# Two attention layers and two routed feed-forward layers on one core: deviation rows by half batch, weight places taken one by one, statistics made ahead by unit

## The chip, the cores and the metric

The kernel runs on one core of a Trainium2 chip. A core has five engines that each work through their own list of instructions in order: TensorE (PE, matrix products and transposes; its weight loads are listed apart as PEld), VectorE (DVE), ScalarE (ACT), GpSimd (POOL) and SyncE (SP), which here issues nearly all DMA transfers. [...]The metric is the time of one execution in microseconds (us) on the device. The kernel before took 4159.81 us (median of 3 runs, 4158.99 to 4161.47).

## The reference, cut to what matters

Four layers work on 4 batches of 4096 tokens with 128 channels. The first two (a state-space scan and a hypergraph layer) are not touched by the change. The other two each consist of an attention and a feed-forward part, both of which read the tokens normalised over their channels:

```python
t = t + _L2_attn_ref(_ln_t(t), L2_attn_W, L2_attn_b)              # causal linear attention
t = t + _L2_ffn_ref(_ln_t(t), gate_w, gate_b, weight1, weight2)
t = t + _L3_attn_ref(_ln_t(t), Wq, bq, Wk, bk, Wv, bv)            # windowed, without softmax
t = t + _L3_ffn_ref(_ln_t(t), gate_w, gate_b, weight1, weight2)

def _ln_t(v, eps=1e-5):
    m = mean(v, axis=-1); s = var(v, axis=-1)
    return (v - m) / sqrt(s + eps)

def ffn(x):                       # 64 experts, 8 tokens each per batch
    probs = softmax(x @ gate_w.T + gate_b, axis=tokens)
    topv, topi = top_k(probs per expert, 8)
    pooled = sum over k of x[topi] * topv                     # (batch, expert, channel)
    h = gelu(pooled @ weight1[expert] + bias)                 # 128 -> 512
    out = h @ weight2[expert] + bias                          # 512 -> 128
    scatter-add out * topv back to the chosen tokens
```

The weights of one feed-forward part are 64 experts times (128 x 512 + 512 x 128) numbers of 4 bytes, 32 MB.

## The kernel before, in words

The tokens of all batches lie in one on-chip tensor `X` (128 tokens by 4 x 32 blocks by 128 channels) from the end of layer 1 on. The order of the work on each engine is that of a list written out by a scheduling layer: it starts from the program's order, but moves an instruction forward into a gap when its inputs and its place are free. So what the source says of an order holds only in part; small VectorE instructions in particular are pulled far ahead.

**attn2** (layer 2, 32 units `u` of one batch and four blocks; `project(u)`, `score(u - 1)`, `attend(u - 2)`). Each unit needs the mean and the deviation of its tokens. `ln_stats` (L733) makes them for 16 blocks, four units, at a time: 16 `bn_stats` on VectorE (L737), some small operations, one Sqrt on ScalarE (L729), a reciprocal. Exp, which every unit needs (L882), and Sqrt lie in different function tables of ScalarE, so each such Sqrt among the units brings two table loads.

**attn3** (layer 3, 32 chunks `s` of one batch and four blocks; `turned(s)`, `gram(s)`, `values(s - 2)`, `mixed(s - 2)`, `put(s - 3)`). Statistics again 16 blocks at a time. Of the four normalised blocks `z` of a chunk ScalarE makes three (L1035) and VectorE one (L1037).

**tokens_done and spread.** As soon as a chunk of tokens has its final value, its `bn_stats` for the feed-forward part are made (L783); 16 blocks are a half batch. `spread` turns a finished half into deviations. Only when all four halves of a pair of batches `p` are there are they transposed, written to a scratch in HBM (L800), and read back as a row that is repeated over 64 experts for each of the two batches (L803, two reads of 1 MB): `rsb[p]`, 128 x 4096.

**ffn.** `logits(p)` works out the gate's logits of a pair in eight chunks and multiplies each by its part of `rsb[p]` (L1198). `choose(p)` marks the eight best tokens (L1215 over all 4096 tokens) and makes the weights by Exp and a product (L1222, L1223). `gather(p)` pools the tokens (L1246, L1253). The order is: `logits(0)`; the last `spread`; `logits(1)` beside `choose(0)`; `choose(1)` beside `gather(0)`; `gather(1)`. Then come 16 groups `g` of four experts: `hidden(g)` with `w1` (L1317), `turn(g - 1)`, `outputs(g - 2)` with `w2` (L1339). `w1` and `w2` of a group are 1 MB each. Five groups have a place on the chip: the first has its own (loaded during the attention), two take the place of the rows `rsb` and two that of `ch` and `ex`, the buffers of `choose`. Each of these two regions is closed as a whole before a load into it is asked for, and group `g + 5` is loaded, `w1` then `w2`, after `outputs(g)`. In layer 3 the steps also transpose `X` back (`channels`, L1360). At last the outputs are scattered into `X` (L1395, L1400; L1405, L1407) and, in layer 3, written out.

Of the kernel before, what the change touches and what calls it, by code (L numbers as in the profile page):

```python
# [41 lines left out]
class Net:  # L42
# [3 lines left out]
    def setup(self, ctx):  # L46
# [22 lines left out]
        self.scratch = [dram.tile([2 * NB, P], F32, tag=f"rs_{i}", name=f"rs_{i}") for i in range(B)]  # L69
# [662 lines left out]
    def ln_stats(self, sp, b, j0, n):  # L732

        nc, X = self.nc, self.X
        st = sp.tile([P, n, 6], F32, tag="lnst", name="lnst")
        for j in range(n):
            nc.vector.bn_stats(st[:, j, :], X[:, b, j0 + j, :])  # L737
        nm = sp.tile([P, n], F32, tag="lnnm", name="lnnm")
        nc.vector.tensor_tensor(nm, st[:, :, 1], st[:, :, 4], ALU.add)
        nc.vector.tensor_scalar(nm, nm, -0.5, None, ALU.mult)  # L740
        rs = sp.tile([P, n], F32, tag="lnrs", name="lnrs")
        self.deviations(sp, st, rs)
        return nm, rs


    def ffn_open(self, name):
# [4 lines left out]
        self.rbp = tc.tile_pool(name="frb", bufs=1, reuse_waits="tile")  # L751
        rbp = self.rbp.__enter__()
# [10 lines left out]
        self.rsb = [rbp.tile([P, N], F32, tag=f"rb{p}", name="rsb") for p in range(B // 2)]  # L763
        self.half, self.halves, self.known = {}, [], [0] * (B // 2)
# [12 lines left out]
    def tokens_done(self, b, c):  # L777
# [4 lines left out]
        for i in range(4):  # L782
            self.nc.vector.bn_stats(self.half[b][:, 4 * k + i, :], self.X[:, b, 4 * c + i, :])  # L783
# [3 lines left out]
    def spread(self, new):  # L787

        nc = self.nc
        for b, h, st in self.halves:  # L790
            p, r = divmod(b, 2)
            self.deviations(self.fsp, st, self.rsk[p][:, r, 16 * h : 16 * (h + 1)])
            self.known[p] += 1
            if self.known[p] == 4:
                pt = new()
                nc.tensor.transpose(pt[: 2 * NB, 0, :], self.rsk[p].rearrange("p r j -> p (r j)"), self.ident)
                rT = self.fsp.tile([2 * NB, P], F32, tag="rT", name="rT", bufs=2)
                nc.vector.tensor_copy(rT, pt[: 2 * NB, 0, :])
                d = self.scratch.pop()
                nc.sync.dma_start(d, rT)  # L800
                for r in range(2):
                    src = bass.AP(tensor=d.tensor, offset=d[r * NB : (r + 1) * NB, :].offset, ap=[[0, E], [1, N]])
                    nc.sync.dma_start(self.rsb[p][r * E : (r + 1) * E, :], src)  # L803
        self.halves = []

    def attn2(self):
# [8 lines left out]
        with ExitStack() as ctx:  # L815
# [28 lines left out]
            state, stats = {}, {}  # L844

            def norms(b, g):
                nm, rs = self.ln_stats(sp, b, G * g, 16)
                nb = sp.tile([P, 16], F32, tag="lnnb", name="lnnb")
                nc.vector.tensor_tensor(nb, nm, rs, ALU.mult)
                nc.vector.tensor_scalar(nb, nb, 1.0, None, ALU.add)  # L850
                stats[b] = rs, nb
                self.spread(new)

            def project(u):

                b, g = units[u]
                if g % 4 == 0:
                    norms(b, g)
                rs, nb = stats[b]
# [3 lines left out]
                for i in range(G):  # L863
                    k = G * (g % 4) + i
                    x, r, m = X[:, b, G * g + i, :], rs[:, k : k + 1], nb[:, k : k + 1]
# [67 lines left out]
            units = [(2 * p + r, g) for p in range(B // 2) for g in range(NB // G) for r in range(2)]  # L933
            S = {}
            for u in range(len(units) + 3):
# [4 lines left out]
                if u < len(units):  # L940
                    project(u)
                if 0 <= u - 1 < len(units):
                    score(u - 1)
# [8 lines left out]
    def attn3(self):  # L952
# [11 lines left out]
        with ExitStack() as ctx:  # L964
# [46 lines left out]
            stats, zts, sums, maps = {}, {}, {}, {}  # L1011

            def norms(s):

# [461 lines left out]
```

## Time and profile before

| | us |
|---|---|
| median of 3 runs | 4159.81 |
| the profiled execution | 4161.4 |
| its span (first to last instruction) | 4159.6 |
| layers 0 and 1, to the start of attn2 | 0 to 3377 |
| attn2 | 3377 to 3644 |
| ffn of layer 2: first transposes of `logits(0)` | 3642.4 |
| its first `hidden` | 3723.8 |
| its first scatter product (L1395) | 3796.4 |
| attn3, first product of a chunk | 3830 |
| ffn of layer 3: first transposes of `logits(0)` | 3970.2 |
| its first `hidden` | 4048.0 |
| its first scatter product (L1405) | 4123.5 |

Busy shares of the whole span: PE 84%, DVE 72%, POOL 59%, ACT 50%. They are an average over very different stages and say little of the last 783 us, which are all that the change touches. How to read the views: the table of stretches gives, for each stretch of time, the busy microseconds and (in brackets) the number of instructions of PE, PEld, DVE, ACT and POOL, then the clock that was granted to PE, the share of the 16 DMA engines' time that was in use and the GB/s they moved. The chain of waits is followed backward from the last instruction: a start, a duration, and what the end was waiting for in that time. A timeline line gives start, duration, engine, source line, operation and operands; in square brackets stands how long the engine had idled before it and for whom. "issue" is time for which the profile shows no cause.

### The profile page before, as it was taken

To read this page: it belongs to the slowest core of one execution; us is meant where nothing else is said; L and a number is where in the kernel's file an instruction comes from. 1 tells how busy PE (TensorE), PEld (TensorE's weight loads), DVE (VectorE), ACT (ScalarE), POOL (GpSimd) and SP (SyncE) were. 2 spreads that over 40 slices of the span, in tenths; PEclk is the share of its full clock that TensorE was granted. 3 is DMA by queue.
4 is the path that set the end of the run, shared out by engine and by line. 5 is a ranking of instruction groups with operands and counts; after the bars stand their busy time and mean duration, and the time that the engine had idled before them with its cause. 6 is when DMAs were issued, how large, how long until landed. Compare 5 with 4: busy or idle time off the path is not lost. (4 is left out here: it accounts for less than half of the span.)

```text
span 4159.6 us, 48628 instructions
## 1 busy us (share of the span) xinstructions
PE 3481.7 (84%) x17232; PEld 1949.8 (47%) x17243; DVE 2985.6 (72%) x4632; ACT 2078.7 (50%) x3519; POOL 2460.1 (59%) x1242
## 2 busy tenths in 40 slices
PE   6878857888888788888967888887998969988988
PEld 2323323444543434445333344543566457855854
DVE  5888889988766899976679988764641077655764
ACT  4556554455644545555444455642124078742941
POOL 5999879888778788877869888773000020001300
PEclk8988978899999889999987999998999989998999
DMA  3445544455446444543644545356111420055037
GB/s 101 149 146 153 157 112 128 132 143 147 115 144 185 111 128 129 153 129 99 218 115 123 137 138 145 114 162 209 59 71 44 139 85 1 22 168 185 22 119 287
DMA packets 263014, 532.71 MB, mean 128 GB/s; under 512 B 22474, under 2 KB 24946, under 8 KB 262258
## 3 DMA queue, kind: packets, MB, share of 16 engines
q1 hardware_dynamic: 254834, 519.08, 42.5%
q10 hardware_dynamic: 7936, 10.52, 0.7%
q8 instruction: 136, 2.23, 0.2%
q14 instruction: 108, 0.88, 0.1%
HBM read 451.80 MB, written 77.73 MB: 127 GB/s over the span
## 5 line engine op out<-in xcount | busy, mean ns | idle before, releaser
L291 POOL TENSOR_TENSOR db<-dx,bt 128x1024 f32<-128x1024 f32 x512 | 1203.2, 2353 | 331.7 <-DVE hs L309 216.0
L309 DVE TENSOR_TENSOR_SCAN hs<-hs,carry,db 128x512 f32<-128x512 f32 x812 | 1037.1, 1285 | 176.9 <-ACT hs L303 94.8
L303 ACT ACTIVATE hs<-dl,A 128x512 f32<-128x512 f32 x1024 | 706.5, 692 | 740.1 <-DVE ho L319 684.9
L326 POOL TENSOR_TENSOR ho_s<-ho_s,ho 128x1024 f32<-128x1024 f32 x288 | 677.9, 2354 | 13.6 <-DVE ho L319 13.0
L504 PE MATMUL ps_g<-xn 128*128 128x512 f32 x1152 | 603.7, 655 | 96.9 <-DVE inc L507 73.3
L319 DVE TENSOR_TENSOR ho<-hs,bt 128x1024 f32<-128x1024 f32 x464 | 564.5, 1217 | 1.6
L527 PE MATMUL ps_ed<-xs,inc 128*128 128x258 f16 x4096 | 516.4, 287 | 18.4 <-ACT inc L520 8.6
L527 PEld LDWEIGHTS <-inc 128*128 128x128 fp8e4 x4096 | 419.0, 103 | 136.3 <-issue 61.1
L507 DVE SCALAR_TENSOR_TENSOR inc<-ps_g,hcl,hb 128x512 fp8e4<-128x512 f32 x576 | 421.8, 739 | 36.9 <-PE ps_g L504 21.5
L504 PEld LDWEIGHTS ps_g<-xn 128*128 128x128 f32 x1152 | 216.1, 204 | 414.5 <-DVE inc L507 180.6
L347 PE MATMUL ps_y<-ho,cst 128*128 128x512 f32 x512 | 274.1, 679 | 108.0 <-POOL ho L315 90.7
L627 PE MATMUL ps_v<-inc_v,es 128*128 128x512 fp8e4 x1536 | 343.3, 383 | 19.3 <-DMA bt<-bcd 17.3
L627 PEld LDWEIGHTS <-es 128*128 128x128 f16 x2048 | 202.7, 99 | 289.7 <-issue 65.1
L520 ACT CAST inc<-ps_t 128x512 fp8e4<-128x512 f32 x448 | 232.2, 599 | 93.7 <-PE ps_t L516 93.5
L229 PE MATMUL ps_c<-xt,wc 128*128 128x512 f32 x512 | 235.4, 614 | 13.0 <-DVE inc L507 6.8
L347 PEld LDWEIGHTS ps_y<-ho,cst 128*128 128x128 f32 x512 | 105.1, 215 | 268.5 <-POOL ho L315 121.6
L533 ACT COPY ed<-ps_ed 128x129 f32<-128x129 f32 x128 | 34.1, 266 | 383.5 <-PE ps_ed L527 383.5
L534 DVE TENSOR_TENSOR ed<-ps_ed,ed 128x129 f32<-128x129 f32 x128 | 36.8, 288 | 212.7 <-ACT ed L533 209.7
L543 POOL TENSOR_TENSOR ed<-ed,rdeg 128x512 f32<-128x512 f32 x32 | 33.3, 1040 | 250.0 <-DVE rdeg L539 250.0
L309 DVE TENSOR_TENSOR_SCAN hs<-hs,db 128x512 f32<-128x512 f32 x116 | 141.4, 1225 | 53.5 <-POOL db L291 42.5
L229 PEld LDWEIGHTS ps_c<-xt,wc 128*128 128x128 f32 x512 | 100.0, 198 | 140.6 <-issue 119.7
L1161 POOL CAST b1h<-b 128x512 bf16<-128x512 f32 x2 | 1.2, 614 | 270.2 <-DMA b<-in_L_ffn_weight 270.2
(321 smaller groups left out, 5493.9 us busy)
## 6 DMA issues: line engine op xcount, KB each, us to landing
bt<-bcd SPq DMA_DIRECT2D x512, 512.0 KB, 5.1
inc<-inc SPq DMA_DIRECT2D x192, 256.0 KB, 2.8
inc_v<-inc SPq DMA_DIRECT2D x96, 512.0 KB, 6.4
w<-in_L_ffn_weight SPq DMA_DIRECT2D x32, 1024.0 KB, 11.5
w2f<-in_L_ffn_weight SPq DMA_DIRECT2D x32, 1024.0 KB, 11.5
strip<-inc SPq DMA_DIRECT2D x84, 256.0 KB, 4.6
x<-x ACTq DMA_DIRECT2D x32, 256.0 KB, 5.5
xn<-x SPq DMA_DIRECT2D x32, 256.0 KB, 5.6
```

What stands on the lines that cost most here:

```text
L229: nc.tensor.matmul(s["ps"][h], wc[:, h, j, :], xt[:, j : j + T], start=j == 0, stop=j == 3)
L291: nc.gpsimd.tensor_tensor(db, s["dx"], bc(s["bt", n][:, 0, :], 2), ALU.mult)
L303: act(nc.scalar.activation(hs[:, k, :], s["dl"][:, k, :], AF.Exp, scale=A[:, k, n : n + 1]))
L309: nc.vector.tensor_tensor_scan(to[:, h, :], hs[:, h, :], db[:, h, :], init, ALU.mult, ALU.add)
L319: nc.vector.tensor_tensor(ho, hs, ct, ALU.mult)
L326: nc.gpsimd.tensor_tensor(s["sum", n // G], s["sum", n // G], ho, ALU.add)
L347: nc.tensor.matmul(s["y"][h], self.ident, t[:, h, :], start=False, stop=n == DS - 1 and k == len(terms) - 1,)
L504: nc.tensor.matmul(pq, xn[v // 4][:, v % 4 * P : (v % 4 + 1) * P], xn[c], start=True, stop=True)
L507: nc.vector.scalar_tensor_tensor(inc[:, v, :], pq, hc[:, v : v + 1], hb, ALU.subtract, ALU.is_gt, saturate=False)
L520: later(1, lambda: act(nc.scalar.copy(inc[:, v, :], pt, saturate=False)))
L527: nc.tensor.matmul(pe[:, : 2 * P + 2], inc[:, v, i * P : (i + 1) * P], xs[:, v, :], start=v == 0, stop=v == NB - 1,)
L627: nc.tensor.matmul(pv, es[:, e, k, :], inc[:, e, :], start=e == 0 and k == 0, stop=e == NB - 1 and k == 1,)
```

## The change

Three things change.

1. A finished half batch becomes its own row at once. `spread` transposes 16 columns instead of 64, writes 16 x 128 numbers and reads them back once, repeated over 64 experts (512 KB). There are four row buffers `rsb[2p + h]` of 128 x 2048, one for each half of each pair, instead of two of 128 x 4096. `logits` takes the half that its chunk lies in.
2. A load of weights takes one place when the last user of that place has ended, not when a region is closed. `w1` and `w2` are loaded by calls of their own. Groups 1 and 2 (modulo 5) take the four row buffers, group 3 takes `ch`, group 4 takes the two `ex` buffers (now two of 128 x 2048 instead of three of 128 x 1024). Group 1 is asked for after `logits(0)` and group 2 after `logits(1)` beside `choose(0)`; `w1` of group `g + 5` is asked for after `hidden(g)`, its `w2` after `outputs(g)`.
3. The attentions' statistics are asked for unit by unit. `measure(n)` makes the `bn_stats` up to unit `n`, `finish(f)` the deviations of a set of units; the sets begin at units 0, 2, 8, 16, 24 in attn2 and at 0, 1, 4, 8, ... in attn3. In attn3 VectorE makes two of the four `z` in even chunks and one in odd ones.

The compiled lists of instructions for layers 0 and 1 are the same in both kernels. In attn2 the list of ScalarE has 13 Sqrt table loads before and 10 after. In both feed-forward parts the list of SP has the two loads of group 1 ahead of the last rows' write and read.

```diff
-    def ln_stats(self, sp, b, j0, n):
-        st = sp.tile([P, n, 6], F32, tag="lnst", name="lnst")
-        for j in range(n):
-            nc.vector.bn_stats(st[:, j, :], X[:, b, j0 + j, :])
...
+    def ahead_of(self, sp, units, firsts):
+        ends = dict(zip(firsts, [*firsts[1:], len(units)]))
+        most = max(e - f for f, e in ends.items())
+        sets, ready, n = {}, {}, 0
+        def measure(upto):
+            nonlocal n
+            while n < min(upto, len(units)):
+                f = max(f for f in firsts if f <= n)
+                if f == n:
+                    st = sp.tile([P, most, 4, 6], F32, tag="lnst", name="lnst", bufs=2)
+                    sets[f] = st[:, : ends[f] - f, :, :]
+                self.block_stats(sets[f][:, n - f, :, :], *units[n])
+                n += 1
+        def finish(f):
+            if f in sets:
+                rs, nb = self.norms(sp, sets.pop(f).rearrange("p u i s -> p (u i) s"))
+                for u in range(f, ends[f]):
+                    i = 4 * (u - f)
+                    ready[u] = rs[:, i : i + 4], nb[:, i : i + 4]
...
-            self.known[p] += 1
-            if self.known[p] == 4:
-                pt = new()
-                nc.tensor.transpose(pt[: 2 * NB, 0, :], self.rsk[p].rearrange("p r j -> p (r j)"), self.ident)
-                rT = self.fsp.tile([2 * NB, P], F32, tag="rT", name="rT", bufs=2)
...
-                nc.sync.dma_start(d, rT)
-                for r in range(2):
-                    nc.sync.dma_start(self.rsb[p][r * E : (r + 1) * E, :], src)
+            pt = new()
+            nc.tensor.transpose(pt[:16, 0, :], self.rsk[p][:, r, 16 * h : 16 * (h + 1)], self.ident)
+            rT = self.fsp.tile([16, P], F32, tag="rT", name="rT", bufs=2)
+            nc.vector.tensor_copy(rT, pt[:16, 0, :])
+            d = self.scratch.pop()
+            nc.sync.dma_start(d, rT)
+            src = bass.AP(tensor=d.tensor, offset=d[0:1, :].offset, ap=[[0, E], [1, N // 2]])
+            nc.sync.dma_start(self.rsb[2 * p + h][r * E : (r + 1) * E, :], src)
...
+            measure(2)
+            finish(0)
             for u in range(len(units) + 3):
...
                     project(u)
+                    measure((5, 8, 10, 11, 12, 14, 15)[u] if u < 7 else u + 9)
+                    finish(u + 1)
+                    if u % 8 == 7:
+                        self.spread(new)
...
-                    if i:
+                    if i % 2 or (i and s % 2):
                         nc.scalar.activation(z[:, i, :], x, AF.Identity, scale=r, bias=m)
                     else:
                         nc.vector.tensor_scalar(z[:, i, :], x, r, m, ALU.mult, ALU.add)
...
+                measure((4, 6, 8)[s] if s < 3 else s + 6)
+                finish(s + 2 if s else 1)
...
-                    nc.vector.tensor_tensor(lg[:, sl], pl, rsb[p][:, sl], ALU.mult)
+                    rb = rsb[2 * p + c // 4][:, c % 4 * CH : (c % 4 + 1) * CH]
+                    nc.vector.tensor_tensor(lg[:, sl], pl, rb, ALU.mult)
...
             run(logits(0))
             self.spread(turned)
+            load(1, 0)
+            load(1, 1)
             second = logits(1)
             next(second)
             run(second, choose(0))
-            self.rbp.__exit__(None, None, None)
-            with_a = ctx.enter_context(tc.tile_pool(name="fe2", bufs=2, reuse_waits="tile"))
-            load(1)
-            load(2)
+            load(2, 0)
+            load(2, 1)
             first = gather(0)
             next(first)
             run(choose(1), first)
-            fctx.close()
-            with_b = ctx.enter_context(tc.tile_pool(name="fe3", bufs=2, side="right", reuse_waits="tile"))
-            load(3)
-            load(4)
+            for g in (3, 4):
+                load(g, 0)
+                load(g, 1)
             run(gather(1))
...
                 if g > 1:
                     outputs(g - 2)
-                    load(g + 3)
+                    if (g - 2) % 5 == 3:
+                        load(g + 3, 0)
+                    load(g + 3, 1)
                 if 0 < g <= NG:
                     turn(g - 1)
                 if g < NG:
                     hidden(g)
+                    if g % 5 != 3:
+                        load(g + 5, 0)
```

## The prediction

> **What bounds the kernel now.** The lists of layers 0 and 1 don't change, so I start with the table of stretches, cut at the stages of the last 783 us.
>
> ```profile
> 3377.00:3640.00 263.00, 241.49 (x1637) 197.79 (x1638) 194.89 (x761) 212.20 (x450) 0.00 (x0) 0.97 0.04 9
> 3662.00:3679.00 17.00, 7.17 (x50) 4.44 (x50) 11.89 (x15) 10.22 (x19) 0.00 (x0) 0.83 0.73 166
> 3679.00:3693.00 14.00, 14.00 (x75) 6.71 (x75) 11.24 (x19) 9.43 (x16) 0.00 (x0) 0.84 0.19 54
> 3724.00:3796.00 72.00, 58.77 (x750) 29.65 (x742) 13.12 (x25) 13.18 (x21) 5.19 (x16) 0.91 0.96 345
> 3830.00:3971.00 141.00, 130.00 (x969) 118.30 (x968) 101.04 (x417) 124.67 (x357) 50.12 (x70) 0.98 0.08 18
> 4048.00:4122.00 74.00, 67.14 (x863) 39.99 (x873) 23.22 (x36) 21.80 (x37) 0.63 (x2) 1.00 0.86 313
> ```
>
> Attn2 (first line) is PE's, with ScalarE behind it. In layer 2's expert groups (fourth line) the DMA share is 0.96: they run at the pace of the weights. In layer 3's (last line) PE comes first and DMA second. Attn3 (fifth line) keeps PE and ScalarE busy together. In the second line PE works 7 of 17 us and the DMA engines are busy: the rows. The chain of waits names these:
>
> ```profile
> 3662.77 2.94 DMA rs<-rT
> 3666.23 11.83 DMA rsb<-rs
> ...
> 3771.38 12.36 DMA w<-in_L_ffn_weight
> ...
> 3790.30 1.98 PE ps_eo L1339 x32
> ...
> 3990.41 11.42 DMA rsb<-rs
> ```
>
> In both feed-forward parts `logits(1)` waits for a write and a read of its rows, and the end of layer 2's groups follows the landing of the last `w1`. VectorE's timeline tells what was really lost to the rows:
>
> ```profile
> 3664.48 4.41 DVE L1215 MATCH_REPLACE8 ch<-m,lg 128x4096 f32<-128x4096 f32 x1
> ...
> 3678.18 1.29 DVE L1198 TENSOR_TENSOR lg<-ps_l,rsb 128x512 f32<-128x512 f32 x2 [4.29 <-DMA rsb<-rs]
> ...
> 3693.30 4.41 DVE L1215 MATCH_REPLACE8 ch<-m,lg 128x4096 f32<-128x4096 f32 x1
> ```
>
> It did `choose(0)` during the wait and idled 4.29 us. From one `MATCH_REPLACE8` to the next are 28.8 us; that stretch is what the rows can shorten. SP's timeline gives the weights' pace:
>
> ```profile
> 3724.95 1.23 SPq L1122 DMA_DIRECT2D w<-in_L_ffn_weight  x2
> 3728.51 2.10 SPq L1125 DMA_DIRECT2D w2f<-in_L_ffn_weight  x2
> ...
> 3771.38 2.54 SPq L1122 DMA_DIRECT2D w<-in_L_ffn_weight  x1
> 3774.01 2.53 SPq L1125 DMA_DIRECT2D w2f<-in_L_ffn_weight  x1
> ```
>
> Issues come 2.6 us apart once the queue is full: 2.6 us for 1 MB, 5.2 us for a group.
>
> **What the Trainium skill says.** "DMA: Bandwidth & Descriptors", section "Anatomy of one DMA — SWDGE (gpsimd) path": about 2.0 us fixed, most of it the receipt of the write, and the bytes at 436 GB/s. That fits here, though SP issues in another way: 32 KB of rows took 1.8 us undisturbed (median), and 1 MB per 2.6 us is 403 GB/s. The same page, "Queues, rings and completion order": each DMA engine takes descriptors in ring order. The rows now stand behind two weight loads on SP's queue, so they wait for them. "ScalarE: Activation LUTs", section "What ACT_TABLE_LOAD costs": 1283 ns for every set, plus a drain of 1380 ns. The trace has 1283 ns as minimum, median and maximum; it shows no such drain (a load at 3458.76 ends as Sqrt begins at 3460.06), so I count 1.29.
>
> **The change part by part.**
>
> *Attn2.* The first norm needs 17 `bn_stats` ahead of it in VectorE's list, after the change 9: 8 x 0.197 us (14 took 2.80, less the last one's latency) = 1.6 us, on the path, since PE idles 7.67 us for the first `z`. The list of ScalarE has three pairs of table loads fewer. A pair is 2 x 1.29 = 2.6 us of ScalarE, but PE has slack against it: steps without a pair take 7.51 us (by the starts of L877), with one 8.15 to 8.47. So 3 x 0.8 = 2.4 us. In steps 1 to 5 (7.1, 7.1, 8.1, 9.5, 8.2 us) VectorE's ahead-made statistics stood before `qk`; with fewer of them I take 1 us. Against it stand eight small transposes of rows where there was one, each behind a reciprocal; PE is the bound here, so they cost between nothing and 0.3 us each if PE has to wait: 1 us at the middle, which cancels the former. Sum -4; ends -8 and +2.
>
> *Rows of layer 2.* What is still missing at the ffn's start are the second halves of batches 2 and 3: two writes, two reads of 512 KB. Chunks 0 to 3 of `logits(1)` find their rows there. VectorE's work from one `MATCH_REPLACE8` to the next: 4.4, four L1223 at 1.15 = 4.6, eight L1198 and eight MAX8 at 0.60 = 9.6, three L1246 at 0.60 = 1.8, small ones 0.5: 20.9 us against 28.8. Now 7.9 of the 28.8 us are idle, 4.3 of them for the rows; of the other 3.6 (MAX8 waits for ScalarE's bias, L1223 for Exp) I keep half, 1.9 us. Gain 6 us; ends 8 and 3. Do the rows come in time? The last product of `logits(0)` ends at 3661.9, so `w2` of group 1 is issued then and holds the queue for 2.6 us, to 3664.6; the writes land 1.8 us later, 3666.4; two reads of 1 MB took 9.7 us (median), of which 2 are fixed, so two of half size 2 + 7.7 / 2 = 5.9: 3672.3, with issue about 3673. Chunk 4's product comes in VectorE's new list after 4.4 + 3 x 0.6 (of chunks 0 to 2) + 1.15 + 3 x 0.6 + 0.6 + 1.15 + 0.6 = 11.5 us: 3676. Three us of margin. The extra transpose, copy and write are 0.1 + 0.2 us, and I count them in the idling. `choose(1)`, `gather` and the first `hidden` follow at unchanged distance (30.5 us), because loads 1 to 4 (8 MB, 21 us) all start earlier than now.
>
> *Groups of layer 2.* Eleven groups, 22 MB, follow the first `hidden`: 22 x 2.6 = 57.2 us, as many as now. Two things are saved. Now `w1` of group 5 is through 2.6 us after 3724.95, and the queue is empty until 3728.51, when `outputs(0)` frees the next place: 1.0 us. In the new list `w1` of group 6 stands between. And at the end, `w1` of group 15 lands at 3783.74, `w2` one transfer later, 3786.3, yet `outputs(15)` starts at 3790.30, behind `hidden(15)` and `turn(15)`. With `w1` asked for two steps earlier these are done, and `outputs(15)` starts as `w2` lands: 4.0 us. Sum -5; ends -6 and -1.
>
> *Attn3.* One of eight `z` goes from ScalarE (0.39 us) to VectorE (0.26): per chunk -0.195 and +0.13. ScalarE is full from 3850 on: three `z` 1.17, `zT` 0.47, `t`, `m` and `G` 0.26 each, the `two` copies 1.43: 3.85 us, with Sqrt about 4.0, of steps of 4.13 (mean of steps 9 to 31). PE's own products are about 3.5. So 0.195 x 23 = 4.5 us, and from the first 8 chunks, which take 5.2 us each while VectorE makes statistics, a half. Sum -5; ends -12 (VectorE's gaps close as well) and +3 (its queue delays `z` and `w`).
>
> *Rows of layer 3.* Only one half row is missing (batch 3): 2 + 2 us of read. VectorE's stretch is the same (3989.9 to 4017.3, 27.5 us against 20.9): -6, ends -7 and -3.
>
> *Groups of layer 3.* Steps are PE's, 4.15 us, except the last four, whose `hidden` come 4.85 us apart (4102.05, 4106.90, 4111.75 in the chain) because 22 MB at 2.6 us, begun at 4049.1, fill the time. With `w1` earlier the queue has fewer gaps (share now 0.86): 4 x 0.7 = -3; ends -5 and 0.
>
> The sum is -4 -6 -5 -5 -6 -3 = -29 us: 4161.4 of the profiled execution becomes 4132. Its time lies 1.6 us above the median of the runs, 4159.8; so **4131** for a median.
>
> **The rivals.**
>
> 1. *The rows come late all the same.* If two loads of 1 MB and the two reads share the rings worse than I think (now a read pair with a load beside it took 11.83 us), chunk 4 waits. From 3 us of delay on, each us costs one, twice. At the pair's present duration they would land at 3678.5, 2.5 us late in layer 2: 4134; wholly as now it is 4131 + 12 = 4143. The order of SP's list speaks for it, the halved bytes against it.
> 2. *The weights' stretch doesn't shorten*, because the queue was never idle in a way that counts, or a new order makes `w2` the late one: 4131 + 8 = 4139. The 0.96 share speaks for it; the 4 us from landing to `outputs(15)` against it.
> 3. *VectorE becomes the bound of attn3, slower than before.* Its work rises by 4 us and statistics for up to six chunks ahead lie in its list before `w` (L1070) and `z`. Chunks 3 to 8 show what that looks like: 5.2 us a chunk. If all 30 kept that pace, attn3 would be 30 x 1.07 = 32 us longer instead of 5 shorter: 4131 + 37 = 4168. It decides from 4.96 us a chunk on, where it eats the other 24 us. Against it: VectorE is busy 101 of 141 us, and the same number of statistics is made today.
> 4. *More than forecast*: attn3 falls to PE's 3.6 us a chunk and attn2 gives 8: 4131 - 12 - 4 = 4115.
>
> That the change doesn't do what it says is rival 1 for the rows; the lists exclude it for the rest.
>
> **How the numbers follow.** A change of less than 0.2%, 8.3 us, can't be told from none by measuring this kernel; faster is below 4151.5. My forecast with its parts off by a few us (4120 to 4142): 0.58. Rivals 1 and 2, singly or together (4134 to 4151): 0.17. Rival 4 (4108 to 4120): 0.12. Rival 3: 0.13, of which 0.04 end below 4151, 0.04 within 0.2% and 0.05 above. So faster 0.88 with roundings, same 0.06, slower 0.06. The range that leaves out some 2 in 10 runs from 4112 to 4148.
>
> **What would show it.** Right: no idling of VectorE at L1217 (the new line of L1198) for `rsb`, about 22 to 23 us between the two `MATCH_REPLACE8`; `outputs(15)` starting within 1 us of the last landing, and first `hidden` to first scatter product 68 us instead of 72.6 in layer 2; chunks of attn3 at 3.9 to 4.0 us; 10 pairs of table loads in attn2. Wrong: a wait of VectorE for `rsb` of several us; chunks of attn3 near 5 us with POOL or PE waiting for VectorE; PE in attn2 waiting for `rsk`'s reciprocal ahead of the small transposes.

## The result, and the profile after

The kernel after takes 4133.85 us (median of 4 runs, 4130.3 to 4139.9); the kernel before took 4160.64 us (median of 4). The ratio is 0.9936, 95% interval 0.9919 to 0.9953. The forecast was 4131, its range 4112 to 4148. The profiled execution is the fastest of the four: 4130.3 us, with a span of 4128.5.

To see where the time went I cut both traces at the same events: the last VectorE instruction of layer 1's normalisation (37 to 38 us follow in which its result is put into `X`), the first `qk`, the first transpose of `X` in each feed-forward part, the two `MATCH_REPLACE8`, the first `hidden`, the end of the last `outputs`, the end of the scatter. The list up to the end of layer 1 is the same in all kernels of this study, yet that part took between 3334.8 and 3349.0 us in their traces. So totals a few us apart say little about one edit, and the stages are compared instead. "Again" is a second trace of the kernel after (an experiment below).

| stage (us) | forecast | before | after | after, again |
|---|---|---|---|---|
| end of layer 1 to the ffn of layer 2 (attn2) | -4 | 303.4 | 296.2 | 296.9 |
| `MATCH_REPLACE8` to `MATCH_REPLACE8`, layer 2 | -6 | 28.8 | 21.7 | 21.7 |
| from there to the first `hidden` | 0 | 30.5 | 29.0 | 30.7 |
| groups of layer 2 | -5 | 68.4 | 65.7 | 65.5 |
| scatter of layer 2 | 0 | 36.4 | 34.7 | 36.2 |
| attn3 | -5 | 141.6 | 140.7 | 140.7 |
| `MATCH_REPLACE8` to `MATCH_REPLACE8`, layer 3 | -6 | 27.5 | 20.5 | 20.5 |
| from there to the first `hidden` | 0 | 30.6 | 29.0 | 29.0 |
| groups of layer 3 | -3 | 72.3 | 70.4 | 70.4 |
| scatter of layer 3 | 0 | 35.5 | 34.3 | 34.3 |
| the rest (both `logits(0)`, the end) | 0 | 45.5 | 45.6 | 45.5 |
| sum | -29 | 820.5 | 787.6 | 791.2 |

The sum fits the forecast better than its terms do. Attn3 gave 0.9 us instead of 5; attn2 and the rows gave more than was forecast; and the gathers and scatters moved, although the change doesn't touch their code. Four traces with one and the same list in attn3 (the two of the kernel after and two experiments elsewhere) took 140.4 to 141.2 us there, so differences of less than about 1 us in that stage say nothing by themselves.

The stretches of the kernel after that answer to those shown of before (first: attn2; then the rows of layer 2, the groups of layer 2, attn3, the groups of layer 3). Columns as before: the stretch, busy time of each engine, the clock that TensorE was granted, DMA share, GB/s.

```profile
3378.00:3636.00 258.00, 241.76 (x1651) 199.15 (x1651) 194.42 (x743) 204.76 (x442) 0.00 (x0) 0.98 0.06 14
3658.90:3680.60 21.70, 21.18 (x127) 10.97 (x128) 20.95 (x32) 17.42 (x30) 0.00 (x0) 1.00 0.59 160
3709.00:3779.00 70.00, 57.99 (x751) 29.94 (x752) 13.91 (x28) 12.97 (x21) 5.25 (x16) 0.95 0.97 356
3811.00:3951.00 140.00, 126.73 (x971) 117.25 (x972) 109.65 (x436) 120.47 (x340) 50.54 (x70) 0.99 0.11 26
4020.00:4092.00 72.00, 67.08 (x863) 40.09 (x872) 23.12 (x37) 21.49 (x37) 0.62 (x2) 1.00 0.89 322
```

In the second line VectorE works 20.95 of 21.70 us: the stretch can get no shorter without less work. In attn3 (fourth line) ScalarE's busy time is 120.5 us where it was 124.7, and VectorE's 109.7 where it was 101.0, and the stage took nearly as long as before.

VectorE's timeline of the kernel after shows the same rows of layer 2 as they were shown of before:

```profile
3658.89 4.41 DVE L1235 MATCH_REPLACE8 ch<-m,lg 128x4096 f32<-128x4096 f32 x1
...
3670.59 0.68 DVE L1217 TENSOR_TENSOR lg<-ps_l,rsb 128x512 f32<-128x512 f32 x1
...
3680.57 4.41 DVE L1235 MATCH_REPLACE8 ch<-m,lg 128x4096 f32<-128x4096 f32 x1
```

L1217 is the line of the old L1198; the one at 3670.59 is that of chunk 4, the first that needs a late half. There is no wait for `rsb`. SP's timeline shows when they came:

```profile
3656.80 0.40 SPq L1140 DMA_DIRECT2D w<-in_L_ffn_weight  x1
3657.57 0.79 SPq L825 DMA_DIRECT2D rs<-rT  x2
3662.53 1.10 SPq L827 DMA_DIRECT2D rsb<-rs  x2
```

The two writes went out at 3657.57, behind `w2` of group 1, and the first landed at 3662.51, right after that load (3662.35). The first read landed at 3667.70. The landing of the second isn't recorded; its last DMA packet ended at 3669.34, and in layer 3 the landing came 0.74 us after the last packet, so about 3670.1 is an estimate. That is only some 0.5 us before chunk 4; in layer 3 the one read landed at 3977.66, 3.2 us before it was needed.

The chain of waits at the end of layer 2's groups:

```profile
3759.64 14.39 DMA w<-in_L_ffn_weight
3774.03 0.14 issue
3774.17 1.12 PE ps_eo L1369 x32
3775.31 0.60 ACT eo L1376
```

The last `w2` lands at 3774.03 and `outputs(15)` starts 0.14 us later. Before, it started 2.06 us after its `w2` (3788.24), behind `hidden(15)` and `turn(15)`.

### The profile page after: what moved, and what is told of

Same layout as the page of the kernel before. It is cut to its first block, busy times and chain, and to the rows that moved or that the text cites. A ratio compares the mean times of both kernels' runs of the same rounds, so it can differ in the third digit from the quotient of the medians.

```text
span 4128.5 us, 48675 instructions
## 1 busy us (share of the span) xinstructions
PE 3469.8 (84%) x17243; PEld 1944.5 (47%) x17255; DVE 2990.9 (72%) x4628; ACT 2065.6 (50%) x3495; POOL 2460.4 (60%) x1242
## 5 line engine op out<-in xcount | busy, mean ns | idle before, releaser
L326 POOL TENSOR_TENSOR ho_s<-ho_s,ho 128x1024 f32<-128x1024 f32 x288 | 677.5, 2352 | 17.4 <-DVE ho L319 16.7
L627 PEld LDWEIGHTS <-es 128*128 128x128 f16 x2048 | 202.4, 99 | 289.5 <-issue 64.4
L533 ACT COPY ed<-ps_ed 128x129 f32<-128x129 f32 x128 | 34.1, 266 | 378.8 <-PE ps_ed L527 378.8
```

The lines of the kernel that those rows point to most:

```text
L326: nc.gpsimd.tensor_tensor(s["sum", n // G], s["sum", n // G], ho, ALU.add)
L627: nc.tensor.matmul(pv, es[:, e, k, :], inc[:, e, :], start=e == 0 and k == 0, stop=e == NB - 1 and k == 1,)
```

## Experiments

Theory: the rows by half batch take the wait out of the two `MATCH_REPLACE8` stretches; the early `w1` takes the chain off the end of the groups; attn2 gains by its sets of statistics; and attn3, against the forecast, is not bound by ScalarE alone. Rivals stand in each expectation. Medians are over 4 to 6 runs, but 20 for the split on the kernel before.

### Who sets the pace of attn3

**The split of z undone**, on the kernel after:

```diff
-                    if i % 2 or (i and s % 2):
+                    if i:
                         nc.scalar.activation(z[:, i, :], x, AF.Identity, scale=r, bias=m)
```

> The kernel after, with three of four z of attn3 on ScalarE in every chunk again. Theory A (the forecast's: ScalarE is the bound of attn3): ScalarE gets 0.195 us more per chunk, attn3 grows from 140.7 us by about 4.5 to 145, the total from 4133.9 to about 4138. Theory B (VectorE's longer list, with its rows by half batch and z, eats what ScalarE gains): attn3 stays within 1.5 us of 140.7, VectorE's busy time in it falls from 110 to about 105 us and ScalarE is the chain again. Theory C (PE is the bound): attn3 stays within 1 us, and ScalarE goes on idling ahead of t and G as it does after.

**The split alone**, on the kernel before: the same line the other way round.

> The kernel before, with one change: in every second chunk of attn3 a second z goes to VectorE. Theory A (ScalarE is the bound): attn3 falls from 141.6 us by 4 to 5, to 137, and the total from 4160 to about 4155.5. Theory B (it is the rest of the change, in VectorE's list, that eats the gain): the same as A here, 137, since the rest isn't in this kernel. Theory C (PE is the bound): attn3 stays at 141 to 142, the total at 4160.

**The statistics of attn3 in sets of 16 blocks again**, on the kernel after (the split stays):

```diff
-            measure(1)
-            finish(0)
+            norms(0)
...
                 if s % 4 == 1:
+                    norms(s + 3)
                     self.spread(new)
...
-                measure((4, 6, 8)[s] if s < 3 else s + 6)
-                finish(s + 2 if s else 1)
```

> The kernel after, with the statistics of attn3 made in sets of 16 blocks at every fourth chunk as before; the split of z and everything else stay. Theory B in its form that the unit-wise statistics cost the gain: attn3 falls from 140.7 to about 137. Otherwise (the unit-wise statistics help, as meant): the first eight chunks go from 31.4 us back to 34, and attn3 grows to 143 to 145.

**More work for one engine**: two of four transposes issued twice (PE), or the first `z` made twice (VectorE):

```diff
-                    nc.tensor.transpose(pt[:, i, :], z[:, i, :], self.ident)
+                    for again in range(2 if i < 2 else 1):
+                        nc.tensor.transpose(pt[:, i, :], z[:, i, :], self.ident)
```

> The kernel after, with two of the four transposes of z in attn3 issued twice: 2 x 0.11 us more of PE in each of 32 chunks, 7.0 us in all, on no other engine. ScalarE's 6.2 us (undone split) cost 1.6 us, a quarter. If PE is the bound of attn3: attn3 grows by 6 to 7 us to 147, total about 4140.5. If no engine is, but the round of G, w, t and m through ScalarE, POOL, VectorE and PE: it grows by 1 to 3 us.

```diff
-                        nc.vector.tensor_scalar(z[:, i, :], x, r, m, ALU.mult, ALU.add)
+                        for again in range(1 if i else 2):
+                            nc.vector.tensor_scalar(z[:, i, :], x, r, m, ALU.mult, ALU.add)
```

> The kernel after, with the first z of every chunk of attn3 made twice on VectorE: about 0.26 us more in each of 32 chunks, 8.3 us in all, on no other engine. If VectorE is the bound of attn3 since the change: it grows by 7 to 8 us to 148, total about 4142. If PE is: by less than 1 us. If none is alone: by 1 to 3 us.

Measured, with the stage cut at the starts of the chunks' transposes ("chunks 8 to 31" is from the start of chunk 8 to that of chunk 31):

| kernel | attn3 | chunks 0 to 8 | chunks 8 to 31 | total, median |
|---|---|---|---|---|
| before | 141.6 | 34.1 | 95.1 | 4160.6 |
| before with the split | 140.5 | 34.3 | 93.6 | 4157.0 |
| after | 140.7 | 31.4 | 96.5 | 4133.9 |
| after, split undone | 142.2 | 33.9 | 95.6 | 4137.1 |
| after, statistics in sets of 16 | 141.8 | 34.1 | 94.9 | 4134.8 |
| after, rows by pair (below) | 139.3 | 31.4 | 95.3 | 4146.6 |
| after, 7.0 us more of PE | 144.9 | 32.7 | 99.2 | 4134.1 |
| after, 8.3 us more of VectorE | 141.7 | 31.8 | 97.1 | 4130.3 |

The totals were taken in several rounds; the kernel before took 4158.3 to 4160.6 us beside them (4159.6 beside the split alone, a ratio of 0.9992, 0.9984 to 1.0000).

Theory A falls. The split alone gives 1.1 us instead of the 4 to 5 that a bound ScalarE would give, and undoing it costs 1.5, not 4.5. Of the pure alternatives none holds either: 7.0 us more of PE cost 4.2 us (0.6 us per us; between the two forecasts of that run), and 8.3 us more of VectorE by the instruction's 0.26 us (10.4 us in VectorE's busy time) cost 1.0, which is hardly more than four traces of one list differ by. In chunks 8 to 31 alone the two cost 2.7 and 0.6. For ScalarE there is no such price: undoing the split also takes work from VectorE, and its 1.5 us come from the first eight chunks (2.5 more) less what the others gain (0.9). So the pace isn't one engine's alone, and of the prices that were measured PE's is the largest. In the steady part PE and ScalarE stood level, as the stretches (before, then after) show:

```profile
3866.00:3959.00 93.00, 88.09 (x671) 80.44 (x670) 63.37 (x251) 88.89 (x257) 31.36 (x45) 1.00 0.11 24
3846.00:3939.00 93.00, 86.68 (x677) 80.53 (x676) 67.42 (x274) 85.14 (x242) 31.24 (x44) 1.00 0.16 36
```

PE's busy time is 88.1 of 93.0 us before, ScalarE's 88.9. The change relieved ScalarE (85.1), and the time did not follow.

The steady part, in which the clock is full in every trace, tells what went against the split. The split takes 1.6 us off chunks 8 to 31 of the kernel before. On the kernel after, undoing the unit-wise statistics gives 1.6 back (96.5 to 94.9), undoing the rows by half batch 1.2 (to 95.3), and undoing the split 0.9 (to 95.6): with the new lists the split costs time there. These figures don't add up (0.9 + 1.6 + 1.2 is more than the 1.4 between before and after), so they are no shares. Which engine is held up isn't shown: VectorE's busy time in these chunks is the same with the statistics in sets of 16 and with the rows by pair (3.1 us a chunk). What attn3 did gain lies in its first eight chunks, 2.7 us, and it takes both: with either the split or the statistics undone they take 34 us again. (That attn3 as a whole then grew by only 1.1 us with the statistics undone, where 2 to 4 were expected, is the steady part's gain.) Part of the 2.7 us may be the clock: in all four traces that took 34 us TensorE had half speed for 6.8 us of these chunks, in the others for 3.4 or for none.

The chain of waits fits a pace that no engine sets alone. Its summary by line for the steady part of attn3 in the kernel before:

```profile
by line: ACT z L1035 27.0%; ACT zT L1039 9.4%; ACT two L1041 8.0%; ACT two L1045 7.9%; ACT G L1056 6.4%; ACT two L1043 6.3%; ACT t L1078 5.7%; ACT m L1087 5.6%; issue 4.4%; ACT two L1040 4.2%; PE ps_t L1076 2.4%; PE ps_g L1055 2.2%; PE ps_o
```

and of the kernel after:

```profile
by line: ACT z L1045 17.3%; ACT zT L1049 8.3%; ACT two L1051 6.5%; PE ps_g L1065 6.4%; ACT G L1066 5.9%; ACT two L1055 5.4%; PE ps_o L1105 5.2%; ACT two L1053 4.6%; POOL w L1079 4.3%; ACT m L1097 4.1%; PE ps_m L1093 4.1%; issue 3.9%; PE ps_
```

Before, the chain runs along ScalarE nearly everywhere; so it was read in the prediction as a bound. But a chain says who ended last, not by how much: PE, as busy as ScalarE, stood right behind. After, the chain changes between ScalarE, PE and POOL.

### Rows

**Rows by pair again**, on the kernel after: one transpose, copy and write when a pair's four halves are known, then four reads of 512 KB.

```diff
+            self.late.setdefault(p, []).append((r, h))
+            if len(self.late[p]) < 4:
+                continue
             pt = new()
-            nc.tensor.transpose(pt[:16, 0, :], self.rsk[p][:, r, 16 * h : 16 * (h + 1)], self.ident)
+            nc.tensor.transpose(pt[: 2 * NB, 0, :], self.rsk[p].rearrange("p r j -> p (r j)"), self.ident)
...
-            nc.sync.dma_start(self.rsb[2 * p + h][r * E : (r + 1) * E, :], src)
+            for r, h in self.late[p]:
+                ...
+                nc.sync.dma_start(self.rsb[2 * p + h][r * E : (r + 1) * E, :], src)
```

> The kernel after, with the rows by half batch undone: one transpose, one copy and one write for a pair of batches, once all its four halves are known, and then four reads of 512 KB. If the wait for the rows was what the stretch between the two MATCH_REPLACE8 lost: it grows in both layers from 21.7 and 20.5 us back to 27 to 29, VectorE idling 4 us or more at L1217's line for rsb, and the total from 4133.9 by 12 to 14 to about 4147. If the new places of the weights, or the loads that now come between, had shortened it: it stays at 21 to 23. A second question is what the rows by half batch cost the attentions: with 7 transposes, copies and writes fewer, attn3 falls from 140.7 us by 1.5 (to 139.2) if they are what was added to it, and by nothing if not; attn2 falls by about 1 from 251.

Measured: 26.3 us between the two `MATCH_REPLACE8` in layer 2 (from 21.7) and 29.0 in layer 3 (from 20.5); total 4146.6, ratio to before 0.9966 (0.9953 to 0.9979) against 0.9936. VectorE's timeline in layer 2 has the wait back:

```profile
3659.93 4.41 DVE L1241 MATCH_REPLACE8 ch<-m,lg 128x4096 f32<-128x4096 f32 x1
...
3671.09 1.29 DVE L1223 TENSOR_TENSOR lg<-ps_l,rsb 128x512 f32<-128x512 f32 x2 [1.74 <-DMA rsb<-rw]
...
3686.22 4.41 DVE L1241 MATCH_REPLACE8 ch<-m,lg 128x4096 f32<-128x4096 f32 x1
```

The wait itself is 1.74 us (3.6 in layer 3); the rest of the growth comes behind it: all eight chunks follow the landing, VectorE waits for products and bias by up to 1.0 us at a time, and of `choose(0)` little is left to fill these gaps. The stretch is the rows', not the weights' places. The second question is answered as well: attn3 fell by 1.4 us to 139.3. Attn2, expected 1 us shorter, came out 0.8 longer up to the ffn, with `logits(0)` 1.2 shorter: 0.4 us between them.

**The first pair whole**: rows by half batch only for the second pair.

```diff
+            if p == 0:
+                ... (the first pair: one transpose, one write, four reads, as above)
+                continue
             pt = new()
             nc.tensor.transpose(pt[:16, 0, :], self.rsk[p][:, r, 16 * h : 16 * (h + 1)], self.ident)
```

> The kernel after, with the rows of the first pair of batches written whole again (one transpose, one write, four reads of 512 KB, long before the ffn), and only those of the second pair by half batch. The seven transposes, copies and writes that the rows by half batch add cost attn3 1.4 us (140.7 against 139.3 with the rows by pair); three of them fall away here: attn3 140.0 to 140.2. If only the last ones, near the ffn, cost anything, it stays at 140.7. The stretches between the MATCH_REPLACE8 stay at 21.7 and 20.5 us, since only the second pair was late. Total 0 to 1.5 us under that of the kernel after.

Measured: attn3 140.4 (-0.3), the stretches 21.7 and 20.5, total 4130.0, ratio 0.9928 (0.9912 to 0.9943). The kernel after beside it has 0.9937: the difference can't be told from none. A 0.3 us gain lies between both expectations, but the stage hides more. Chunks 8 to 31 took 95.5 us, against 96.5 in the kernel after and 95.3 with the rows by pair: there most of the rows' cost goes with the first pair's steps. The first eight chunks, whose lists are the same in all three, took 32.1 here and 31.1 to 32.0 in four traces of the kernel after's list.

### Weights

**w1 asked for together with its w2**, on the kernel after:

```diff
-                    if (g - 2) % 5 == 3:
-                        load(g + 3, 0)
+                    load(g + 3, 0)
                     load(g + 3, 1)
...
-                    if g % 5 != 3:
-                        load(g + 5, 0)
```

> The kernel after, with w1 of a group asked for together with its w2, behind the outputs of the group whose place it takes, as before; the places stay. The groups of layer 2 take 65.4 to 65.8 us after, 66.3 and 68.4 in two traces with the old order; those of layer 3 70.4 and 72.3. Theory: the stream of 22 MB has a fixed length of 63.3 us (64.2 in layer 3) from the first release to the last landing in either order, and what the early w1 saves is the chain behind the last landing: hidden and turn of group 15. Then here groups of layer 2 take 66.5 to 68.5 and those of layer 3 72.3, total about 4138, and the stream stays at 63 to 64. My forecast's: the stream itself gets 1 us longer as well, 64.3. Rival: the new places alone made the groups shorter; then nothing changes here.

Measured: groups 66.4 us (65.7) in layer 2 and 72.3 (70.4) in layer 3, and the scatter of layer 3 35.6 (34.3); total 4136.5. From the first `w` issue behind the first `hidden` to the last landing, and from there to the end of the last `outputs`:

| | layer 2: stream, behind it | layer 3: stream, behind it |
|---|---|---|
| before | 63.3, 4.0 | 64.2, 7.0 |
| before with the split | 63.4, 1.8 | 65.1, 6.0 |
| after | 63.3, 1.2 | 64.3, 4.9 |
| after, w1 with w2 | 63.4, 1.8 | 64.4, 6.8 |

In layer 2 the stream has one length in every order (63.1 to 63.4 us in all 14 traces), and the early `w1` takes work from behind its end: `outputs(15)` starts 0.14 us after the last landing in all eleven traces with the new order, and 0.72 us after it in two with the old. That is worth 0.6 us; the other 2.2 us of before were a clock of 0.5, granted from 3782.3 on in that trace.

In layer 3 the last landing sets nothing: it comes 3.7 to 5.9 us before `outputs(15)` starts, and while the streams of the traces range from 63.9 to 65.1 us, the groups take 72.3 us in all three with the old order and 70.4 in all eleven with the new. PE waits there for ScalarE's activation between `hidden` and `turn`, not for weights. First a line of the old order (this run), which occurs four times from `hidden(12)` on, then one of the kernel after, whose list puts `hidden(13)` and `hidden(14)` side by side:

```profile
4085.78 0.65 PE L1358 MATMUL ps_t<-cst,h 128*128 128x128 f32 x4 [0.78 <-ACT h L1352]
...
4078.85 1.90 PE L1347 MATMUL ps_h<-w,pooled 128*32 128x512 f32 x16
```

With every wait counted PE idles 3.9 us in the last steps of the old order and 2.3 in the new: 1.6 of the 1.9 us. The 1.2 to 1.3 us in the scatter of layer 3 belong to the order by way of the clock: its list of instructions is the same in every kernel, but in the three traces with the old order (35.5 to 35.6 us) TensorE had half speed for 3.4 us, beginning 3.3 to 3.8 us after the last `outputs`, and in the eleven with the new (34.3) it hadn't. The chain of the kernel with the old order, at the end of layer 3's groups:

```profile
4093.22 0.90 PE ps_h L1347 x8
...
4094.20 0.60 ACT h L1352
...
4094.85 0.67 PE ps_t L1358 x4
4095.54 0.70 DVE hT L1360
...
4096.29 1.12 PE ps_eo L1369 x32
```

After the last landing (4090.55) there follow, one behind the other, `hidden(15)`, its activation, `turn(15)`, its copy and the last `outputs`.

### Attn2

**The statistics of attn2 as before**, on the kernel after (`norms(b, g)` at the first of four units, 16 blocks of one batch, with its call of `spread`; no `measure`, no `finish`):

```diff
-            measure, finish, ready = self.ahead_of(sp, units, [0, 2, 8, 16, 24])
...
-                rs, nb = ready.pop(u)
+                if g % 4 == 0:
+                    norms(b, g)
+                rs, nb = stats[b]
```

> The kernel after, with the statistics of attn2 as before: 16 blocks of one batch at a time, at the first of four units. My forecast gave attn2 4 us, and the stretch to the first qk and from there to the ffn is 7.2 us shorter in the trace after. If the statistics are the cause: first qk 46.7 us after layer 1's end instead of 45.1, attn2 256 to 257 us instead of 251, 13 pairs of table loads instead of 10, total about 4141. If the rows by half batch or something else had made attn2 shorter: attn2 stays at 251 to 252 and the total at 4134 to 4135.

Measured: the first `qk` 46.5 us after layer 1 instead of 45.1, 257.8 from there to the ffn instead of 251.1, total 4139.5. So the sets are worth 8.1 us up to the ffn, and about 7 with `logits(0)`, which is 1.3 us shorter here. What the rows by half batch cost attn2 isn't shown: 0.9 us by this run against before (304.3, 303.4), but 0.8 in their favour by the rows by pair above, and with `logits(0)` counted 0.4 or 0.5 us either way. The first norm is seen best from the last copy into `X` to the first `qk`: 9.35 us in the three traces with the old statistics and 7.81 in the eleven with the new. ScalarE's groups of the kernel after in this stage:

```profile
L897 ACT ACT_TABLE_LOAD x10 | 12.8, 1283 | 0.2
L729 ACT ACT_TABLE_LOAD x10 | 12.8, 1283 | 0.2
```

and with the statistics undone:

```profile
L920 ACT ACT_TABLE_LOAD x13 | 16.7, 1283 | 0.2
L729 ACT ACT_TABLE_LOAD x13 | 16.7, 1283 | 0.2
```

By the starts of `qk`, the 6.7 us after the first one are, with steps counted from 0: 2.4 in steps 6 to 31 (where the table loads are fewer; that these are the whole cause isn't shown), 2.8 in steps 2 to 5 (8.14, 9.46, 8.15, 7.54 us against 7.25, 8.57, 7.52, 7.19), and 1.6 in step 1, which took 7.12 or 5.55 us. That last one is the clock (0.76 or 1.00 in it). The list of before has both values in two traces (7.12 in the kernel before, 5.55 with the split in attn3); all eleven traces with the new statistics have 5.55, so whether the list helps the clock there stays open.

### The clock, and a better version

**The kernel after, unchanged, once more**:

> The kernel after, unchanged, once more on the same chip as the three beside it, for comparison. If the gather (29.0 us in its first trace, 30.5 to 30.7 in most of the others with the same lists there) and the scatter of layer 2 (34.7 against 36) take one of two values by the clock that PE is granted, and not by the change, one or both of them can come out at the longer value here: the part of the time after layer 1 is then 789 to 793 us instead of 787.6. All stages without a drop of the clock agree within 0.3 us with the first trace.

Measured: 4132.8 us (median of 6), ratio 0.9937 (0.9923 to 0.9951); in the trace 791.2 us after layer 1, the gather of layer 2 30.7 us and its scatter 36.2. The stretches of the gather in the first trace of the kernel after:

```profile
3690.20:3695.10 4.90, 3.37 (x58) 2.88 (x54) 3.21 (x9) 0.00 (x0) 0.00 (x0) 1.00 1.03 376
```

and at the same place in the second:

```profile
3697.00:3702.10 5.10, 4.46 (x52) 4.22 (x50) 2.16 (x6) 0.00 (x0) 0.00 (x0) 0.67 1.03 375
```

A clock of 0.67 over 5.1 us is half speed for 3.4 us. Cut finer, with the 3.4 us ahead of it, the second trace shows:

```profile
3694.70:3698.10 3.40, 1.30 (x20) 1.06 (x22) 3.40 (x6) 0.00 (x0) 0.00 (x0) 1.00 0.70 202
3698.10:3701.50 3.40, 3.40 (x36) 3.40 (x34) 1.06 (x3) 0.00 (x0) 0.00 (x0) 0.50 1.02 372
```

The Trainium skill, "TensorE: Matmul & The Clock Gate", section "What's actually happening", gives the mechanism: the gate halves the clock after an idle window of about 3.4 us and opens it after a busy one, and the windows run freely, without regard to when the kernel starts. The length agrees: half speed lasts 3.41 us or a small multiple of it in all the stretches looked at here. But the window ahead of this one wasn't empty, PE worked 1.3 of its 3.4 us. So one list has two times in the gather of layer 2, 29.0 and 30.7 us, by where a window falls while PE waits for VectorE's `MATCH_REPLACE8`; in layer 3 there are values between (29.8, 30.0) as well. The 1.5 us that the first trace gained in each gather are not shown to be an effect of the change: the four gathers with the old list took 30.5 to 30.7, of 24 in the other traces nine took 29.0. The scatter of layer 2 took 34.6 to 37.4 us in the traces with the kernel after's lists there, and 34.6 or 34.7 in just the three without half speed in it.

**The one-row copies of attn3 on POOL**, on the kernel after:

```diff
-                nc.scalar.copy(two[c][lo, 1, :], z[lo, 0, :])
+                nc.gpsimd.tensor_copy(two[c][lo, 1, :], z[lo, 0, :])
...
-                    nc.scalar.copy(two[c + 1][lo, 0, :], z[lo, 2, :])
+                    nc.gpsimd.tensor_copy(two[c + 1][lo, 0, :], z[lo, 2, :])
```

> The kernel after, with the two one-row copies into two in attn3 on POOL instead of ScalarE: ScalarE gets 0.28 + 0.30 us less per chunk, 18 us in all, POOL as many instructions more. By the measured price of ScalarE's time in this stage (undoing the split: 6.2 us of ScalarE cost 1.6 us of time; the split alone on the kernel before: 6.2 us gained 1.1) attn3 falls by 3 to 4.5 us to about 137, total about 4130. Rival: POOL's sums w, on the round that PE waits for, come later behind the copies, and attn3 grows by 1 to 5 us.

Measured: attn3 135.8 us (-4.9), total 4124.7 (median of 5, 4124.6 to 4127.3), ratio to before 0.9918 (0.9905 to 0.9932). The 60 copies had taken 17.4 us of ScalarE, so one us bought 0.28: a little more than the 3 to 4.5 us expected. That expectation rested on the undone split as ScalarE's price, which in the steady part had the other sign; that it came near is in part luck. POOL had the room, since it idles most of the stage waiting for `G`. The chain by line in its attn3:

```profile
by line: PE ps_g L1065 15.9%; PE ps_o L1105 14.6%; PE ps_t L1086 9.7%; PE ps_g L1076 8.7%; PE ps_m L1093 7.9%; PE ps_z L1048 6.8%; DVE lnst L735 5.0%; DVE fst L735 4.3%; DVE w L1080 4.2%; DVE X L1107 3.3%; DVE z L1047 2.4%; POOL w L1079 2.4
```

Now the chain runs mostly along PE, at 4.02 us a chunk (chunks 8 to 31), of which PE is busy 3.79. By the lesson above that doesn't make PE a bound; no run tests it here.

**Both edits**, the first pair whole and the copies on POOL:

> Both edits of the two kernels beside it: the first pair's rows whole, and the one-row copies on POOL. If they add: attn3 136 to 137, total 4 to 5 us under the kernel after. If POOL becomes the late one in either, they don't add, and attn3 is that of the copies on POOL alone.

Measured: attn3 135.4 us, 0.4 under the copies alone (0.5 in chunks 8 to 31, where the first pair whole had given 1.0): they add in part at most. The total is 4129.5 (median of 6), ratio 0.9930 (0.9915 to 0.9944). That it isn't below the 4124.7 lies outside the stages: its traced part after layer 1 took 787.0 us against 786.8, and the part up to the end of layer 1 took 3349.0 against 3336.0 us.

## Why the prediction came out as it did

*The total* was right: -26.8 us by the medians against -29. That it came so near is in part luck. Attn2 and the rows held in mechanism and gave up to 5 us more than was forecast; attn3 and the groups of layer 2 gave some 6 to 8 less; the groups of layer 3 became shorter for another reason than the one forecast, and the scatter behind them added 1.2 us that no term has.

*Attn2* (-4; 7.2 in the trace, of which 1.6 is the clock's). The first norm's 1.6 us came as 1.5 (9.35 to 7.81 us from the last copy into `X`), and the steps that hold the table pairs' 2.4 gave 2.4. The rows' transposes, taken as 1 us, can't be told from nothing. Mis-sized was the term of the early steps: 2.8 instead of 1.

*Rows* (-6 and -6; -7.1 and -7.0). Right in mechanism and nearly in size. The work of 20.9 us was exact; of the 1.9 us of idling that I kept, 0.8 was left. The landing was mis-sized. It was forecast for 3672.3 to 3673 by the clock of before, which is 5.6 us ahead there: 3666.7 to 3667.4. It came at about 3670.1: the writes landed 1.7 us later than forecast (3662.5 instead of 3660.8), since a load of 1 MB takes 5.1 to 5.6 us to land even when it stands alone (group 1's two here), not 2.6, and the two reads took 7.6 instead of 5.9 (an earlier such pair in the same trace 6.8). The margin was about 0.5 us instead of 3: rival 1 stayed out, but narrowly.

*Groups of layer 2* (-5; -2.8 in the trace, 0.6 by the order alone). Two steps of it failed. The 1.0 us of an empty queue was misread: the row that the prediction shows says x2 at 3724.95, so `w1` of group 6 stood there before the change too, and the stream has its gap and its 63.3 us (put at 57.2) in both. And the 4.0 us at the end: `w2` of group 15 was put at 3786.3 but landed at 3788.24, so only 2.06 us of waiting lay behind it, and with a full clock 0.72. That `outputs(15)` would follow the landing at once was right (0.14 us). Rival 2, no shortening because the queue is full, was right about the stream and wrong about its end.

*Attn3* (-5; -0.9). The step that failed is "ScalarE is full from 3850 on", and with it 0.195 x 23 = 4.5 us. ScalarE was one of several: the split alone took 1.6 us off chunks 8 to 31 of the kernel before. "PE's own products are about 3.5" was no measure of how far PE stood behind; its busy time was 3.9 us of a chunk's 4.13, like ScalarE's, and the lowest pace of any run here, with ScalarE relieved of three times as much, is 4.0. Besides, the other new lists cost time in chunks 8 to 31 (1.6 us the statistics by unit, 1.2 the rows by half batch, each by undoing it), which the prediction counted at nothing there; a chunk took 4.20 us instead of the 3.9 to 4.0 named as a sign of being right. Rival 3, VectorE as the bound, was wrong as a bound (8 to 10 us more of its work cost 1.0 us; 4.2 us a chunk instead of 4.96); whether it was right that VectorE's queue delays `w` and `z` isn't shown. The half that I gave to the first eight chunks was 2.7 us.

*Groups of layer 3* (-3): -1.9 there and -1.2 in the scatter behind. The size was near, the reason was wrong: the last `hidden` came 4.85 us apart because PE waited 0.78 us for each one's activation, not because the loads fill the time. The early `w1` let the list hide two of these waits, and that the scatter got a full clock was not foreseen.

*What else wasn't in the sum*: the gathers and the scatter of layer 2, 4.9 us in the trace, gone in part in its repetition. They go with the clock.

## What to carry to other kernels

A chain of waits that runs along one engine doesn't make that engine a bound: before a relief is counted in full, ask how far the next engine stands behind, from its own busy time. Adding a known amount of work to one engine at a time prices each of them; an edit that moves work from one engine to another prices neither. A stage that ends with a stream of loads is as long as the stream and what must come after the last landing, but only if something waits for that landing: layer 2's groups did, layer 3's looked the same and didn't. And a clock that differs between two traces is not always chance: the scatter of layer 3 has one clock with the old order of loads and another with the new, in all 14 traces.

## What was not expected of the hardware

One and the same list takes 29.0 or 30.7 us in the gather, and 5.55 or 7.12 us in a step of attn2, by a TensorE clock of half speed for some 3.4 us that falls on the path or beside it. In the trace shown it follows 3.4 us in which PE was busy for 1.3, so it doesn't take an empty window. A copy of one row of 128 takes POOL 0.29 us and ScalarE 0.28 to 0.30: such small pieces take no longer on POOL. The full queue moves 386 GB/s (2.71 us per MB), in both kernels and in every order tried, while one load alone takes 5.1 us and more from issue to landing.
